# Head channels in the even rows of a slot: one transfer for the slots of four heads

## The chip, the cores and the metric

The kernel runs on one core of a Trainium2 chip. The metric is the device time of one execution in microseconds (us); the time before is the median of three runs. A profile is one execution recorded by the hardware profiler; its span runs from the first to the last recorded instruction.

## The reference

The layer has four sequences of 1024 positions with 256 channels. Cut to what matters here:

```python
def attention(x, w_attn, w_proj):             # 16 heads of 16 channels
    q, k, v = split(x @ w_attn.T)
    att = einsum("bhqd,bhkd->bhqk", q, k) / sqrt(16)
    att = att + where(rel <= 0, slope[h] * rel, -inf)   # rel = key position - query position
    return (softmax(att) @ v) @ w_proj.T

x = x + attention(layernorm(x))
x = x + encoder_layer(layernorm(x))  # attention over the 4 sequences at each position,
                                     # router, one of 8 experts per row, two norms
```

The change lies in the first attention, in how a score `q k` gets its position term `slope * rel`.

## The kernel before

**Slots.** A group is four of the 16 heads. For each group there is a tile `slots[g]` of 128 partitions; each head has 32 of them, its slot. The first 256 columns are queries, the other 1024 are keys. The first 16 rows of a slot (D = 16) hold the head's channels. The rows after them hold what the scores add: row 16 carries the key's position against a constant in the queries, row 17 a constant against the query's position, and rows 18 to 25 one row for each block of 128 positions, by which scores of the second half of a block's keys with the first half of its queries, all above the diagonal, are pushed down. One matmul over the 32 rows of a slot gives a head's scores with the position term included. `key_rows` and `query_rows` write these rows with VectorE and GpSimd operations on all 128 partitions; they use small tables made at the start: `at_row` (1 in row 16), `is_one` (1 in row 17), `at_block`, `steep`, `k_by` (from the slopes) and `q_by` (the slopes in row 17, loaded by four small transfers).

**Units and stages.** The work is cut into chunks of 256 queries (c = 0 to 3) for each of the four sequences; a unit is one chunk of one sequence, and in the last chunk 128 queries, so there are 20 units. A unit needs the keys of its own and all earlier chunks, so stage c has 256(c+1) key columns. For each unit and group, `score` makes the scores on TensorE (tile `sk`), ScalarE takes the exponential (`p`), GpSimd cuts the diagonal block, and `weigh` multiplies by the values (`pv`).

**Filling a slot.** `project_qk` makes queries and keys of two groups at once (tile `qkp`, copied by VectorE into `kq`) and stores them to `k_of` in device memory. `fill_slots(u, g)` then copies the channels of the four heads into the slots, straight from `kq` in stage 0 and from `k_of` afterwards. The 64 channel rows of a group are consecutive in the source, but in the slots there are gaps of 16 rows after every 16, so it takes four transfers, one for each head. They are issued on SP, for the first unit every second one on ScalarE. A fill of group g for unit u+1 stands in the program right after the last scores of group g in unit u.

**Order.** The order of instructions is written by the program: slots E and D between the scores take the projections and the next part of the layer, with due times from a small cost table. Each engine works in its own order. SP's queue holds, in program order, the stores of `k` and `y`, the fills, the loads of `x`, and for each unit after its attention a chain: load the softmax sums (`load_sums`), VectorE inverts them (`invert`), store them (`r`), load them spread over channels (`load_inverse`, tile `su`), VectorE multiplies (`divide`, tile `yc`), then `project` multiplies by `wp` on TensorE. In stage 0 the `y` stores are issued by ScalarE.

PSUM has four pairs of banks that go round: scores, products and projections take them in turn, so a score waits until the reader of an earlier tile in its pair is done.

Of the kernel before, what the change touches and what calls it, by code (L numbers as in the profile page):

```python
# [33 lines left out]
ALU = mybir.AluOpType  # L34
# [3 lines left out]
P = 128  # L38
B, T, C = 4, 1024, 256
H, D, E = 16, 16, 8  # L40
S = 32
G = H // 4
# [4 lines left out]
W = 256  # L47
# [34 lines left out]
IDENT, MASK_Q, MASK_K, K_ROWS, SLOPES, Q_ROW, IOTA, EARLIER = (  # L82
    0, P, 2 * P, 3 * P, 3 * P + T, 3 * P + T + G, 3 * P + T + G + 1, 3 * P + T + G + 1 + E,
)
# [522 lines left out]
def fast_layer(ctx: ExitStack, tc: tile.TileContext, odd, x, wq, wk, wv, wp, w_in, w_out, w_r,  # L607
# [26 lines left out]
    nc = Core(tc.nc, told)  # L634
# [14 lines left out]
    def const(name, shape, dtype=F32, into=keep):  # L649
        return into.tile(shape, dtype, tag=name, name=name)  # L650
# [45 lines left out]
    con = lambda at, n=1: low_con[:, at - SLOPES:at - SLOPES + n]  # L696
# [7 lines left out]
    load_x(2)  # L704
    q_by = const("q_by", [P, G])
    nc.vector.memset(q_by, 0.0)
    for j in range(4):
        r = j * S + D
        nc.scalar.dma_start(q_by[r + 1:r + 2], consts[r:r + 1, SLOPES:SLOPES + G])
    mask = fact.tile([P, P], F32, tag="sc", name="mask")  # L710
    nc.scalar.dma_start(mask, consts[:, MASK_Q:MASK_Q + P])
    wp_sb = load("wp", wp, [P, CC, C], into=ends)
# [17 lines left out]

    minus_half = const("minus_half", [P, 1])
    nc.vector.memset(minus_half, -0.5)
    at_row = con(Q_ROW)
    number_i = const("number_i", [P, 1], I32)
    nc.gpsimd.iota(number_i, pattern=[[0, 1]], base=0, channel_multiplier=1)
    pos = fact.tile([P, T], F32, tag="pr", name="pos")
# [11 lines left out]
    number = const("number", [P, 1])  # L748
    nc.vector.tensor_copy(number, number_i)
    own_e = const("own_e", [P, 1])  # L750
    nc.vector.tensor_copy(own_e, own_e_i)
    is_one = const("is_one", [P, 1])
    nc.vector.tensor_scalar(is_one, number, float(D + 1), None, ALU.is_equal)


    at_block = const("at_block", [P, NT])
    steep = const("steep", [P, NT])
    for i in range(NT):
        nc.vector.tensor_scalar(at_block[:, i:i + 1], number, float(D + 2 + i), None, ALU.is_equal)
    nc.vector.tensor_scalar(steep, at_block, STEEP, None, ALU.mult)  # L760
    other = const("other", [P, 1])
    k_by = const("k_by", [P, G])
    nc.vector.tensor_scalar(other, at_row, 4.0, None, ALU.mult)
    nc.vector.tensor_scalar(k_by, con(SLOPES, G), other, None, ALU.mult)
    nc.vector.tensor_scalar(other, at_row, -1.0, 1.0, ALU.mult, ALU.add)


    slots = [const(f"slots{g}", [P, W + T], into=pad) for g in range(G)]
# [11 lines left out]
    def query_rows(c, g):  # L780

        qt = slots[g][:, :W]
        nc.vector.tensor_scalar(qt, q_pos, float(c * W), other, ALU.add, ALU.mult)
        nc.vector.tensor_scalar(qt, qt, at_row, q_by[:, g:g + 1], ALU.add, ALU.mult)
        if g == 0:
            for n in range(PC):
                early = qt[:, n * P:n * P + P // 2]
                i = PC * c + n
                nc.vector.tensor_scalar(early, early, steep[:, i:i + 1], None, ALU.add)
# [47 lines left out]
    k_of = [dram.tile([C, W + T], F32, tag=f"k_{b}", name=f"k_{b}") for b in range(B)]  # L837
# [10 lines left out]
    sums, at = [], 0  # L848
# [4 lines left out]
    held = {}  # L853
# [8 lines left out]
    def issue_stores(*keys, age=None):  # L862
        due = [it for it in stores if it[0] in keys or age is not None and it[1] >= age]
        for it in due:
            stores.remove(it)
            it[2]()
# [77 lines left out]
    def fill_slots(u, g):  # L944

        n, i, _ = units[u]
        c, b = batches[n]
        if b == 0 and c and i == 0:
            query_rows(c, g)
        for j in range(4):  # L950
            at, row_ = slice(j * S, j * S + D), (4 * g + j) * D
            n_cols = W + (c + 1) * W
            issue_stores(("k", n, g // 2))
            src = k_of[b][row_:row_ + D, :n_cols]
            if c == 0:
                row_ = (4 * (g % 2) + j) * D
                src = held["kq", n, g // 2][row_:row_ + D].rearrange("p k w -> p (k w)")
            queue = nc.scalar if u == 0 and j % 2 else nc.sync
            queue.dma_start(slots[g][at, :n_cols], src)

    def blocks_of(u, r):

# [159 lines left out]
    slot_sum = const("slot_sum", [P, P])  # L1122
    nc.gpsimd.memset(slot_sum, 0.0)
    for j in range(4):
        at = slice(j * S, (j + 1) * S)
        nc.gpsimd.tensor_copy(slot_sum[at, at], at_row[at].to_broadcast([S, S]))

    def load_slotted():
        held["wp"] = []
# [918 lines left out]
    queue, running = [], []  # L2048
# [93 lines left out]
    def slots_of(n, half):  # L2142
        return lambda: [fill_slots(n, 2 * half + k) for k in range(2)]

    for u, (n, i, size) in enumerate(units):
        c, b = batches[n]
# [77 lines left out]
    for g in range(G):  # L2224
        at_E(-8, lambda g=g: key_rows(g, 0, W, nc.vector if g else nc.gpsimd))
        at_E(1 + g, lambda g=g: key_rows(g, W, T, nc.vector if g else nc.gpsimd))
    at_E(-5, lambda: [fill_slots(0, g) for g in range(2)])
    at_E(-3, lambda: [fill_slots(0, g) for g in range(2, G)])
    at_E(4, prepare)
    at_E(6, part.prepare)  # L2230
# [152 lines left out]
    def begin(it):  # L2383
        if it.kind == "DQ" and ("qkv",) in held or it.kind[1:] == "C" and part.placed < NT - 1:
            return 1e9
        return max(it.ready, free[engine_of[it.kind[0]]])
# [27 lines left out]
    while threads:  # L2414
# [4 lines left out]
        at, _, it = min((begin(it) + FIRST_BY * n, n, it) for n, it in enumerate(threads))  # L2419
# [14 lines left out]
    n = 0  # L2434
# [11 lines left out]
@with_exitstack  # L2446
def tile_layer(ctx: ExitStack, tc: tile.TileContext, *args):
    nc = tc.nc
    flag = ctx.enter_context(tc.tile_pool(name="flag", bufs=1))
    odd = flag.tile([P, 1], I32, tag="odd", name="odd")  # L2450
    fast_layer(tc, odd, *args)
    again = nc.values_load(
        odd[0:1, 0:1], min_val=0, max_val=1,
        skip_runtime_bounds_check_because="a comparison's result",
    )
    with tc.If(again > 0):
        general_layer(tc, *args)
# [75 lines left out]
```

## Time and profile before

| | |
|---|---|
| median of three runs | 805.2 us (803.28 to 805.44) |
| the profiled execution | 802.74 us, span 801.0 us |
| TensorE busy | 710.5 us (89%) |
| VectorE, ScalarE, GpSimd busy | 521.5, 433.0, 254.1 us |
| mean granted TensorE clock | 0.966 |
| transfers into slots on SP | 56 of 32 KB from `kq`; 64 of 48 KB, 64 of 64 KB, 128 of 80 KB from `k_of` |
| transfers into slots on ScalarE | 8 of 32 KB from `kq` |

In the profile's lines a group is given as line, engine, operation, output<-inputs and count; busy time and idle time before it follow. "L588" is a helper through which all instructions of TensorE, VectorE and ScalarE are issued, so these are told apart by their tiles. Names ending in q (SPq, ACTq) are an engine's sequencer: it waits or issues a transfer. A line of the chain of waits gives a start, a duration and what it was; a transfer's duration there runs from its issue to its landing.

### The profile page before, as it was taken

To read this page: it belongs to the slowest core of one execution; us is meant where nothing else is said; L and a number is where in the kernel's file an instruction comes from. 1 tells how busy PE (TensorE), PEld (TensorE's weight loads), DVE (VectorE), ACT (ScalarE), POOL (GpSimd) and SP (SyncE) were. 2 spreads that over 40 slices of the span, in tenths; PEclk is the share of its full clock that TensorE was granted. 3 is DMA by queue.
4 is the path that set the end of the run, shared out by engine and by line. 5 is a ranking of instruction groups with operands and counts; after the bars stand their busy time and mean duration, and the time that the engine had idled before them with its cause. 6 is when DMAs were issued, how large, how long until landed. Compare 5 with 4: busy or idle time off the path is not lost.

```text
span 801.0 us, 22678 instructions
## 1 busy us (share of the span) xinstructions
PE 710.5 (89%) x9029; PEld 538.2 (67%) x9029; DVE 521.5 (65%) x1282; ACT 433.0 (54%) x663; POOL 254.1 (32%) x360
## 2 busy tenths in 40 slices
PE   4889869999998999999889999899998687979993
PEld 3666656666666666666568877578777466868882
DVE  7245324747887574889672338588689788865553
ACT  1455525745556565556547657458467163646650
POOL 5443202312222120114221211123112230788874
PEclk9799979999999999999999999999999999999997
DMA  7344444343344332325354545246431660444420
GB/s 221 98 155 139 144 136 136 121 117 110 84 141 126 109 123 76 100 80 155 89 161 139 134 142 170 76 132 173 122 116 52 186 255 27 135 130 123 127 86 26
DMA packets 75220, 99.57 MB, mean 124 GB/s; under 512 B 19496, under 2 KB 58723, under 8 KB 74596
## 3 DMA queue, kind: packets, MB, share of 16 engines
q1 hardware_dynamic: 62272, 67.84, 28.8%
q10 hardware_dynamic: 7972, 16.05, 6.4%
q0 software_dynamic: 4864, 14.16, 5.9%
q8 instruction: 74, 1.21, 0.7%
q14 instruction: 38, 0.31, 0.1%
HBM read 61.55 MB, written 35.12 MB: 121 GB/s over the span
## 4 chain that ended last, share of the span: by engine, by line
PE 53%; DVE 20%; DMA 8%; issue 7%; POOL 6%; ACT 3%; SPq 1%; ACTq 0%; POOLq 0%; DVEq 0%
PE sk L588 14%; PE pv L588 11%; PE qkvp L588 9%; PE qkp L588 6%; PE vp L588 5%; DVE pv L588 4%; POOL given L1852 3%; ACT p L588 2%; PE oe L588 2%; DVE sc L588 2%; PE op L588 2%; DVE pr L588 1%; PE ao L588 1%; DVE u L588 1%; DMA out_dram<-o,out_rows 1%
## 5 line engine op out<-in xcount | busy, mean ns | idle before, releaser
L588 ACT ACTIVATE p<-sk 128x1024 f32<-128x1024 f32 (+1 forms) x320 | 287.4, 940 | 157.8 <-PE sk L588 138.5
L1006 POOL TENSOR_SCALAR_AFFINE_SELECT p<-p 128x512 f32<-128x512 f32 (+1 forms) x160 | 105.6, 664 | 426.9 <-ACT p L588 424.9
L588 PE MATMUL sk<-slots 32*128 32x128 f32 (+1 forms) x3456 | 180.8, 328 | 23.5 <-issue 9.5
L588 PEld LDWEIGHTS sk<-slots 32*128 32x128 f32 x3456 | 137.0, 188 | 65.8 <-issue 31.8
L588 PE MATMUL pv<-p,v 128*32 128x128 f32 (+1 forms) x3456 | 143.4, 313 | 10.3 <-ACT p L588 4.0
L588 PEld LDWEIGHTS pv<-p,v 128*32 128x32 f32 x3456 | 95.6, 110 | 47.9 <-ACT p L588 7.8
L588 PE MATMUL qkvp<-w_in,ut 128*128 128x264 f32 (+1 forms) x240 | 85.1, 493 | 0.2 <-ACT ut L588 0.2
L588 PEld LDWEIGHTS qkvp<-w_in,ut 128*128 128x128 f32 x240 | 43.1, 193 | 29.6 <-issue 24.8
L588 PE MATMUL qkp<-xt,wqk 128*128 128x256 f32 x224 | 56.2, 396 | 0.2 <-ACT p L588 0.2
L588 PEld LDWEIGHTS qkp<-xt,wqk 128*128 128x128 f32 x224 | 41.4, 193 | 10.9 <-issue 3.3
L588 ACT ACTIVATE mt<-mtp,columns 128x128 f32<-128x128 f32 x76 | 30.7, 455 | 30.6 <-PE mtp L588 30.6
L588 DVE COPY kq<-qkp 128x512 f32<-128x512 f32 x28 | 19.1, 683 | 43.1 <-PE qkp L588 42.7
L588 PE MATMUL hid<-mt,w 128*128 128x128 f32 x304 | 44.6, 283 | 2.6 <-ACT ge L588 1.7
L1852 POOL DMA_INDIRECT given<-rows,rows x38 | 42.1, 1108 | 9.7 <-issue 8.5
L588 PEld LDWEIGHTS hid<-mt,w 128*128 128x128 f32 x304 | 40.0, 191 | 3.8 <-ACT ge L588 2.2
L588 DVE COPY vr<-qkvp 128x264 f32<-128x264 f32 x28 | 12.1, 432 | 46.3 <-PE qkvp L588 46.3
L1967 POOL DMA_INDIRECT out_dram<-o,out_rows x38 | 39.2, 1033 | 8.7 <-issue 5.9
L588 ACT COPY qkv<-qkvp 128x512 f32<-128x512 f32 x28 | 16.4, 585 | 46.8 <-PE qkvp L588 46.7
L588 PE MATMUL oe<-w,ge 128*128 (+1 forms) x152 | 40.0, 386 | 0.0
L588 DVE TENSOR_TENSOR pv<-vr,sc 128x1024 f32<-128x1024 f32 x32 | 39.6, 1238 | 0.3
L588 DVE TENSOR_REDUCE sc<-pr 128x64 f32<-128x1024 f32 x32 | 39.0, 1220 | 1.1
L588 DVE TENSOR_TENSOR pr<-qkv 128x1024 f32<-128x1024 f32 x32 | 39.2, 1224 | 0.5 <-ACT qkv L588 0.2
(317 smaller groups left out, 1038.4 us busy)
## 6 DMA issues: line engine op xcount, KB each, us to landing
slots<-k SPq DMA_DIRECT2D x128, 80.0 KB
k<-kq SPq DMA_DIRECT2D x32, 256.0 KB
v<-v ACTq DMA_DIRECT2D x4, 1152.0 KB
x<-in_x_dram SPq DMA_DIRECT2D x16, 256.0 KB
y<-yt SPq DMA_DIRECT2D x16, 256.0 KB
rows<-x SPq DMA_DIRECT2D x32, 128.0 KB
slots<-k SPq DMA_DIRECT2D x64, 64.0 KB
rows<-u SPq DMA_DIRECT2D x8, 512.0 KB
```

Source lines behind the costliest of these rows:

```text
L588: ins = made(*args, **kwargs)
L1006: nc.gpsimd.affine_select(blocks, blocks, pattern=[[0, 2], [0, size], [1, P]], compare_op=ALU.is_ge, fill=0.0, base=0, channel_multiplier=-1,)
L1852: nc.gpsimd.indirect_dma_start(out=self.hx, out_offset=None, in_=t.rows_of, in_offset=bass.IndirectOffsetOnAxis(ap=t.rows_[:, self.j:self. ...
L1967: ins = nc.gpsimd.indirect_dma_start(out=out.rearrange("t n c -> (t n) c"), out_offset=bass.IndirectOffsetOnAxis(ap=t.table.out_rows[:, t. ...
```

## The change

The channels of a head move to the even rows of its slot, row 2d for channel d, and what the scores add moves to odd rows: the key position to row 1, the constant and the slopes to row 3, the eight blocks to rows 5 to 19. The channels of four heads are then 64 rows at a step of two in the slots and 64 consecutive rows in the source, and `fill_slots` makes one transfer. In the first unit the transfers go by group, not by head, to SP and ScalarE in turn. The tables follow: `at_row` is now made by a comparison on VectorE (the old one, a column of the constants, stays as `sum_row` for the sums), the slopes are loaded into rows 1 (`slopes`, used for `k_by`) and 3 (`q_by`) by two transfers of four rows each in place of four transfers of one row.

```diff
-    for j in range(4):
-        r = j * S + D
-        nc.scalar.dma_start(q_by[r + 1:r + 2], consts[r:r + 1, SLOPES:SLOPES + G])
+    slopes = const("slopes", [P, G])
+    nc.vector.memset(slopes, 0.0)
+    for t, r in ((slopes, 1), (q_by, 3)):
+        nc.scalar.dma_start(t[r:P:S], consts[D:P:S, SLOPES:SLOPES + G])
...
-    at_row = con(Q_ROW)
+    sum_row = con(Q_ROW)
...
-    is_one = const("is_one", [P, 1])
-    nc.vector.tensor_scalar(is_one, number, float(D + 1), None, ALU.is_equal)
+    at_row, is_one = const("at_row", [P, 1]), const("is_one", [P, 1])
+    nc.vector.tensor_scalar(at_row, number, 1.0, None, ALU.is_equal)
+    nc.vector.tensor_scalar(is_one, number, 3.0, None, ALU.is_equal)
...
-        nc.vector.tensor_scalar(at_block[:, i:i + 1], number, float(D + 2 + i), None, ALU.is_equal)
+        nc.vector.tensor_scalar(at_block[:, i:i + 1], number, float(5 + 2 * i), None, ALU.is_equal)
...
-    nc.vector.tensor_scalar(k_by, con(SLOPES, G), other, None, ALU.mult)
+    nc.vector.tensor_scalar(k_by, slopes, other, None, ALU.mult)
...
-        for j in range(4):
-            at, row_ = slice(j * S, j * S + D), (4 * g + j) * D
-            n_cols = W + (c + 1) * W
-            issue_stores(("k", n, g // 2))
-            src = k_of[b][row_:row_ + D, :n_cols]
-            if c == 0:
-                row_ = (4 * (g % 2) + j) * D
-                src = held["kq", n, g // 2][row_:row_ + D].rearrange("p k w -> p (k w)")
-            queue = nc.scalar if u == 0 and j % 2 else nc.sync
-            queue.dma_start(slots[g][at, :n_cols], src)
+        n_cols = W + (c + 1) * W
+        issue_stores(("k", n, g // 2))
+        src = k_of[b][4 * g * D:4 * (g + 1) * D, :n_cols]
+        if c == 0:
+            row_ = 4 * (g % 2) * D
+            src = held["kq", n, g // 2][row_:row_ + 4 * D].rearrange("p k w -> p (k w)")
+        queue = nc.scalar if u == 0 and g % 2 else nc.sync
+        queue.dma_start(slots[g][0:P:2, :n_cols], src)
```

More of the change, by code (lines that the diff above doesn't have):

```diff
@@ L1125, in fast_layer @@
         at = slice(j * S, (j + 1) * S)
-        nc.gpsimd.tensor_copy(slot_sum[at, at], at_row[at].to_broadcast([S, S]))
+        nc.gpsimd.tensor_copy(slot_sum[at, at], sum_row[at].to_broadcast([S, S]))
     def load_slotted():
```

## The prediction

> **What bounds the kernel now.** I read the slices of the page first, then the groups, the table of waits, the chain of waits, and last the timeline of single engines around every hole in TensorE's work.
>
> ```profile
> PE   4889869999998999999889999899998687979993
> PEclk9799979999999999999999999999999999999997
> ACT xt L588 <- DMA slots<-kq: 11.7, 1, 11.7
> DVE yc L588 <- DMA su<-r: 18.4, 5, 11.6
> SPq L959 <- PE sk L588: 120.8, 53, 12.4
> L959 SPq DMA_DIRECT2D slots<-k x256: 302/370/1787, 83.0 to 600.3; - x128
> L959 SPq DMA_DIRECT2D slots<-kq x56: 507/539/2519, 17.2 to 74.1; - x56
> ```
>
> TensorE (the first line; a slice is 20 us) is full from about 110 to 600 us and has its holes before 110 us and after 600. The clock line shows lower digits in the same early slices. The three lines of the waits name what is late: transfers into the slots at the start, and once a load of `su` that kept VectorE waiting 11.6 us. The last two lines are the issues that the change touches: 312 on SP, each 0.37 or 0.54 us long, in one queue with every store and load of the attention.
>
> The chain of waits, and the timelines of SP, VectorE and TensorE, at the holes:
>
> ```profile
> 2.31 5.12 DMA q_by<-in_consts_dram
> 24.26 1.65 PE sk L588 x10
> 68.60 3.61 DMA k<-kq
> 72.29 0.39 ACTq L588
> 73.65 1.45 PE sk L588 x10
> 83.43 2.15 DMA slots<-k
> 86.52 1.96 PE sk L588 x15
> ...
> 69.59 5.04 SPq L959 DMA_DIRECT2D slots<-kq  x8
> 83.00 4.40 SPq L959 DMA_DIRECT2D slots<-k  x8
> 96.04 4.30 SPq L959 DMA_DIRECT2D slots<-k  x8
> 100.44 0.37 SPq L1085 DMA_DIRECT2D r<-inverse  x1
> 103.29 1.33 SPq L1096 DMA_DIRECT2D su<-r  x2
> 107.00 0.69 DVE L588 TENSOR_TENSOR yc<-yc,su 128x512 f32<-128x512 f32 x1 [11.62 <-DMA su<-r]
> 107.61 0.68 DVE L588 COPY kq<-qkp 128x512 f32<-128x512 f32 x1
> 108.39 2.20 PE L588 MATMUL sk<-slots 32*128 32x256 f32 x16 [6.76 <-issue]
> ```
>
> Three holes hang on SP's queue. (1) At 72 us ScalarE sits at the issue of a `y` store until the `k` store of 68.60 has landed (72.21), though the two share no data: in the program as built the transfers of SP and ScalarE take eight completion semaphores in turn, and an issue waits until the holder before it has landed. Its exponentials start at 72.79, and TensorE stands 1.71 us for a bank. (2) At 84.45 TensorE stands 2.06 us until the first fills of the second stage land; SP came to them late, through 16 fills and their neighbours. (3) At 101.63 TensorE stands 6.76 us: `r` is issued only behind eight fills (100.44), `su` after it has landed, the division on VectorE waits for `su`, and the copy of `kq` queued behind it frees the bank that the scores need.
>
> **The change, part by part.** *SP's queue.* 256 fills from DRAM at a pitch of 0.43 us and 56 from `kq` at 0.63 become 64 and 14: 192 x 0.43 + 42 x 0.63 = 109 us less of issuing. By itself that is worth nothing, since SP waits 121 us for scores anyway; it counts where SP is behind, which is in the three places. An issue of 64 rows does not occur before; the nearest are those of 16 rows (0.37, 0.54) and the stores of `k`, 128 rows (0.33 to 0.53); I take 0.45. Its landing lies between the 2.15 us of a 16-row fill and the 3.61 us of a `k` store that was delayed; I take 2.5 us, against 1.3 + 2.15 = 3.5 us until the last of four staggered fills.
>
> *Hole 1.* With 8 fills fewer between them, the holder before the `y` store landed long ago. 1.71 us of standing go. The clock goes with them: the granted clock was 0.50 from 73.9 to 77.3, in which 32 `pv` took 2.60 us (1.51 elsewhere) and 12 `sk` 1.45 (0.70): 1.8 us more. Gain 3.5.
>
> *Hole 2.* From 61 to 83 us SP issues 16 fills (10 us); as four at 0.5 they leave SP some 6 us ahead, less what `kq`'s second half makes it wait (copied at 66.5), so about 4: the fills are issued near 76.5 and land near 79, while TensorE, 3.5 us ahead, asks at 81. Gain 2.06 of standing and, at 0.50 of the clock after it, 1.0 on `sk` (1.96 for 0.94) and 1.25 on `vp` (3.24 for 1.99): 4.3.
>
> *Hole 3.* I walk SP on: fills done 77; three `b_bf` 79.3, `sums` and `yc` 81.2, three `in_bf` 83.1, `k` store 83.6, landed 86; two fills 86.7; `r` 87, landed 89; `su` lands 92.3; division 93, copy of `kq` 93.7. TensorE, with its own work between from the timeline (93.30 to 101.63, moved by the 7.8 us of holes 1 and 2), asks at 93.8. So next to nothing of the 6.76 stays; I leave 0.3. In the before, 104.6 to 114.9 ran at 0.50: `sk` 2.20 for 0.94, eight `vp` 3.78 for 1.99, four transposes 0.97 for 0.60, 3.4 us. Gain 9.9. If `su` is later than I walk, each us of it costs one.
>
> By the Trainium skill (TensorE: Matmul & The Clock Gate, section Why this matters for your kernels) only gaps over about 3 us bring the slow clock. The trace does not agree: holes of 1.71 and 2.06 us were each followed by 3.4 us at 0.50. By that rule the sum would be about 4 us smaller.
>
> *The start.* In unit 0 the last fill of group 0 is held until 21.16 by the semaphore of a `b_rows` transfer and lands at 24.2; the scores end at 25.9. After, that group is one transfer, and ScalarE issues two fills for eight (6.2 us there). Against it stands a new wait: `k_by` now reads `slopes`, which comes where the first `q_by` row came, behind the 512 KB of `wk` on ScalarE's queue, and that row landed at 7.43; `k_by` ran at 3.82. Behind it on VectorE are queued `row_no`, `places`, the statistics of `x_0` and then `xn`, on which the first transposes wait. They move from 7.45 to about 10.4, 2.9 us, and all up to the transposes at 19.14 with them; these end at 23.4, the fill (issued 20.2) has landed by 22.7, the scores run to 25.05. Gain 0.9; bounds: 2.9 gain if `slopes` does not lie behind `wk`, 2.1 loss if it lands 3 us later than `q_by` did.
>
> *With one answer.* `at_row` by a comparison (0.15 us) and a memset of `slopes` (0.06) lie in VectorE's 1.15 us of waiting for `low_con`; without that cover they cost 0.2. Two issues fewer on ScalarE at 2.31 gain nothing, the table load has 2 us of slack. Comparisons with 5 + 2i cost what those with 18 + i did. `slot_sum` reads the old constant column. Matmuls keep 32 rows and their order, so TensorE's own work stays.
>
> *Later.* The holes at 211, 384 and 416 us wait for VectorE's own work. At 500.1 (2.72 us) the fills lie behind a 1152 KB load of `v`; all four landed just after it, and one transfer will too. The tail after 620 us starts earlier by the whole gain.
>
> Sum: 3.5 + 4.3 + 9.9 + 0.9 = 18.6. I take off 1.6 for new small waits, since the 6.8 us of hole 3 were also time in which the other engines caught up (the groups show VectorE fed by TensorE with single waits up to 9.6 us): 17. The profiled execution took 802.74 us (span 801.0 and 1.7 around it), so 785.7. It lies 2.5 under the median of 805.2 and 0.5 under the fastest run; the median should come to 788.
>
> **The rivals.** *Part of it (793 to 802).* The copies of `kq` are held by VectorE's own chain rather than by `su`, or hole 2 moves on to the transfer of one `k` store; then hole 3 gives 4 or less and the sum is 3 to 12. For: VectorE waits in that stretch for several transfers in turn (`sums` 4.8, `b_bf` 2.1). Against: in hole 3 it was idle for 11.6 us.
>
> *Nothing (803 to 807).* SP only runs ahead to the next score it must wait for. For: 120.8 us of such waits. The Trainium skill (DMA: Bandwidth & Descriptors, section Issuing engines are not separate DMA queues) states that the time to issue is usually small relative to the transfer. Here eight issues take 4.3 us against 2.15 us of one landing, so it is not small in this queue. Against: no wait for a score stands between the fills and `r` in hole 3.
>
> *Slower (806 to 810).* The wait of `k_by`. It costs 2.9 us before the first transpose; it decides if the holes at 72 to 108 us are not SP's: then the start stands alone, and it turns from a gain of 0.9 to a loss once `slopes` lands after 8.3 instead of 7.43; 3 us later makes it 2.1, and the half clock after the longer hole up to 3 more. For: nothing covers it. Against: the first scores waited until 24.26 for fills.
>
> *The change does not do what it says*: 64 partitions at a step of two could be served as slowly as four transfers one after the other, 4 x 2.15 = 8.6 us to land. Fills have a unit's time (14 us in the first stage, over 25 later) after the score that frees the slot, so only holes 2 and 3 would stay: 797 to 802, inside the first rival.
>
> **How the numbers follow.** Forecast (783 to 793) 0.63; part 0.20; nothing 0.06; slower 0.11. A measurement of this kernel can tell about 0.3%, 2.4 us, from no change, so faster begins under 802.8: 0.83, within 0.06, slower 0.11. The range reaches from 781, if the start gains its 2.9 and `su` and all else fit, to 802, the end of the partial case.
>
> **What would show it.** In the profile after: 64 + 14 fills on SP at 0.3 to 0.6 us; `k_by` at about 7.5 and the first `xn` at about 10.4; the first scores done by 25; no hole over 1 us in TensorE between 60 and 100 us, and a granted clock of 1.00 there; the score that stood at 108.39 near 93; SP's waits for scores above 120.8 us, since it arrives earlier. The prediction is wrong if hole 3 stays above 3 us, if a new hole of that size opens before 200 us, or if fills land later than 4 us after their issue outside the big `v` loads.

## The result: 785.8 us for 805.3

The changed kernel takes 785.76 us (median of four runs, 784.45 to 786.16), the kernel before 805.32 on the same chip (four runs, 803.28 to 806.1): 19.5 us less, a ratio of 0.976 (95% interval 0.974 to 0.978). The forecast was 788 in a range of 781 to 802. The profiled execution took 784.45 us (span 782.7), 18.3 less than that of before.

The page of after, its slices (one of 40 is now 19.6 us):

```profile
PE   3889899999999999998989999999997879879992
PEclk9999899999999999998999999999999898999997
```

TensorE's 6 in the sixth slice is a 9 now and the 8 in the fifth has stayed; the clock's 7 in the second and in the sixth slice are gone, and an 8 in the fifth is new (80 to 87 us). By windows of 60 to 110 us TensorE was busy 39.5 us at a mean granted clock of 0.88 before, and 47.9 us at 0.93 after. From the tables of waits of after (all in us: in total, how often, the longest):

```profile
ACT p L588 <- DMA b_bf<-pieces: 6.3, 2, 4.6
DVE yc L588 <- DMA su<-r: 6.0, 4, 3.3
SPq L961 <- PE sk L588: 149.7, 39, 13.7
```

VectorE's wait for `su` is down from 18.4 to 6.0 us, and SP waits longer for scores (149.7 for 120.8), as it does when it comes earlier. The first line is new: exponentials that wait 4.6 us for a bias transfer. The fills, by the line that issues them (shortest, median and longest issue in ns):

```profile
L961 SPq DMA_DIRECT2D slots<-k x64: 450/487/753, 75.3 to 576.0; - x64
L961 SPq DMA_DIRECT2D slots<-kq x14: 462/519/708, 19.9 to 64.7; - x14
```

The timelines of SP, ScalarE, VectorE and TensorE at the places of holes 2 and 3:

```profile
76.55 2.57 SPq L1505 DMA_DIRECT2D b_bf<-pieces  x3
85.58 1.13 SPq L961 DMA_DIRECT2D slots<-k  x2
86.80 0.54 SPq L1087 DMA_DIRECT2D r<-inverse  x1
89.38 1.30 SPq L1098 DMA_DIRECT2D su<-r  x2
...
79.78 0.34 ACTq L588 DMA_DIRECT2D v<-v  x1
80.22 1.51 ACT L588 ACTIVATE p<-sk 128x768 f32<-128x768 f32 x2 [4.61 <-DMA b_bf<-pieces]
...
93.05 0.69 DVE L588 TENSOR_TENSOR yc<-yc,su 128x512 f32<-128x512 f32 x1 [1.53 <-DMA su<-r]
94.36 0.69 DVE L588 COPY kq<-qkp 128x512 f32<-128x512 f32 x1 [0.62 <-PE qkp L588]
...
81.08 2.08 PE L588 MATMUL sk<-slots 32*128 32x256 f32 x12 [2.07 <-ACT p L588]
97.22 1.15 PE L588 MATMUL sk<-slots 32*128 32x256 f32 x16
```

Hole 3 is closed: the last line is the score that stood at 108.39 behind 6.76 us of idle time; it comes 2.2 us after the copy of `kq` has ended (94.36 + 0.69) and waits for nothing. The hole that waited for fills is gone, but four matmuls further on there is one of the same 2.07 us with another cause (called hole 2 all the same below). A load of `v` on ScalarE (`load_values`, for the second stage), issued at 79.78, takes over the completion semaphore of a `b_bf` transfer that lands at 79.76, and the exponentials queued behind that load start at 80.22. TensorE waits for the bank that they read.

Counting TensorE's matmuls (9029 in each profile) shows where the time came from. The table gives how much earlier the n-th starts after than before; the predicted terms stand beside their stretches. The last column is the same count on a second profile of each kernel (`before2` and `after2` below):

| up to matmul | earlier by, us | of this stretch | predicted | of this stretch, second pair |
|---|---|---|---|---|
| 400 (start; 59.8 us after) | 2.0 | 2.0 | 0.9 | -0.8 |
| 600 (hole 1) | 6.1 | 4.0 | 3.5 | 4.4 |
| 700 (hole 2) | 4.4 | -1.7 | 4.3 | -0.3 |
| 900 (hole 3) | 14.3 | 10.0 | 9.9 | 8.0 |
| 5000 (447.7 us after) | 16.8 | 2.4 | no gain, less 1.6 | 3.8 |
| 6000 (the hole at 500 us before) | 21.4 | 4.6 | 0 | 5.5 |
| 9000 (tail) | 18.3 | -3.1 | 0 | 0.8 |

Two executions stand behind each pair, so a row carries the accidents of both. Hole 1, hole 3 and the hole at 500 us give a gain in both pairs, hole 2 in neither; the start and the tail change sign.

### The profile page after: what moved, and what is told of

Read it like the earlier page. It is cut to its first block, busy times and chain, and to the rows that moved or that the text cites. A ratio compares the mean times of both kernels' runs of the same rounds, so it can differ in the third digit from the quotient of the medians.

```text
span 782.7 us, 22121 instructions
## 1 busy us (share of the span) xinstructions
PE 705.6 (90%) x9029; PEld 535.4 (68%) x9029; DVE 523.5 (67%) x1284; ACT 433.3 (55%) x663; POOL 256.9 (33%) x360
## 5 line engine op out<-in xcount | busy, mean ns | idle before, releaser
L1008 POOL TENSOR_SCALAR_AFFINE_SELECT p<-p 128x512 f32<-128x512 f32 (+1 forms) x160 | 107.8, 678 | 401.1 <-ACT p L588 399.0
L588 PE MATMUL sk<-slots 32*128 32x128 f32 (+1 forms) x3456 | 177.6, 327 | 8.9 <-DVE kq L588 4.2
L588 PEld LDWEIGHTS sk<-slots 32*128 32x128 f32 x3456 | 134.6, 187 | 51.0 <-issue 21.2
L588 PE MATMUL qkvp<-w_in,ut 128*128 128x264 f32 (+1 forms) x240 | 83.5, 486 | 0.2 <-ACT ut L588 0.2
```

The source lines that it names most:

```text
L588: ins = made(*args, **kwargs)
L1008: nc.gpsimd.affine_select(blocks, blocks, pattern=[[0, 2], [0, size], [1, P]], compare_op=ALU.is_ge, fill=0.0, base=0, channel_multiplier=-1,)
```

## The experiments

The runs were made in three groups, each on one chip, and the kernel before was slower or more scattered there than above (medians 813.7, 807.7 and 804.9 us). So a ratio is to the before of its own group, and kernels of one group are compared with each other.

**Four transfers in the new layout.** This keeps rows, tables and the two transfers saved at the start, and undoes only the number of fills. `e2_unit4`, `e3_unit16` and `e9_from5` are the same edit with `u == 4`, `u == 16` and `u >= 5` in place of `True`.

```diff
+        if True:
+            for j in range(4):
+                queue = nc.scalar if u == 0 and j % 2 else nc.sync
+                queue.dma_start(slots[g][j * S:(j + 1) * S:2, :n_cols], src[j * D:(j + 1) * D])
+            return
         queue = nc.scalar if u == 0 and g % 2 else nc.sync
         queue.dma_start(slots[g][0:P:2, :n_cols], src)
```

> The kernel after, with its rows and tables, but with four transfers of 16 rows for a group again (in the first unit every second one on ScalarE). If the gain is the number of issues, SP's queue is as full as before: 803 to 807 us, a ratio of 1.000 to the kernel before, and the 6.8 us hole near 102 us and the 2.7 us hole near 500 us are back. If it comes from where the rows lie, from the tables or from the two transfers saved at the start, it stays at 784 to 790.

Measured: 820.3 us, a ratio of 1.009 (1.006 to 1.012). The gain is the number of issues, and the new layout with as many issues as before is a loss, which neither theory had. The line of the fills in its profile:

```profile
L963 SPq DMA_DIRECT2D slots<-k x256: 485/539/1726, 79.5 to 611.6; - x128
```

An issue of 16 rows at a step of two takes 0.54 us where one of 16 adjacent rows took 0.37 (median, from `k_of`): 256 x 0.17 = 43 us more in SP's queue. That this is the whole of the loss is not shown. The three early holes are back, with 2.4, 1.8 and 7.35 us, and new holes of 2.6 and 4.0 us opened at 136 and 243 us. One issue of 64 rows at a step of two takes 0.49, less than one of 16.

> The kernel after, with four transfers for a group in unit 4 alone (the first of the second stage): 12 issues more of 240, some 5 us of SP's time between 75 and 90 us. If the holes of 84 and 102 us come from SP's backlog at this place, su lands about 5 us later (near 98 instead of 92.97), the division and the copy of kq with it; TensorE asks for the bank at about 97, so a hole of about 3 us opens there, and the clock falls after it: 4 to 8 us more than after, 790 to 794 (ratio 0.981 to 0.986). If issues cost the same wherever they stand, 12 of 240 cost 5% of 19.5 us, 1 us: 786.8 (0.977).

Measured: 803.9 us, 0.987 (0.981 to 0.993), 11 us more than `e3_unit16` in the same group (792.9), which stands for after there; the first theory had 4 to 8. VectorE and TensorE, at the place of hole 3:

```profile
103.44 0.69 DVE L588 TENSOR_TENSOR yc<-yc,su 128x512 f32<-128x512 f32 x1 [14.07 <-DMA su<-r]
...
96.75 1.54 PE L588 MATMUL sk<-slots 32*128 32x256 f32 x12 [3.59 <-ACT p L588]
104.83 2.20 PE L588 MATMUL sk<-slots 32*128 32x256 f32 x16 [3.88 <-issue]
```

`su` landed at 103.3, 10 us later than after, not 5: beside the issues themselves SP stood from 89.1 to 93.1 until a `k` store had landed. The 3.59 us are a `y` store of ScalarE that waited for the landing of one of these fills (95.12). From matmul 600 to 900 this kernel lost 10 us against `e3_unit16`. Twelve issues of 240 cost about half of the whole gain at this place (11 of the 20.8 us between before and `e3_unit16`), where the count alone gives 5%; the price is that of the place. Hole 2 was not there: the load of `v` went out at 76.11, ahead of the bias transfers.

> The kernel after, with four transfers for a group in unit 16 alone, the one whose fills stood beside a 1152 KB load of v at 493 us before. If four small transfers beside the load make both slow (8.8 us for the load before, 5.5 after), the load beside the second group's fills takes 8 to 9 us again, a hole of 2 to 3 us opens near 482 us, and the time is 3 to 5 us more than after: 789 to 791 (ratio 0.979 to 0.982). If it was only the chance position of the load among other transfers, as the prediction's 'one transfer will too' has it, nothing changes by over 1 us: 785 to 787.

Measured: 792.9 us, 0.973 (0.969 to 0.977), not to be told from after. The load of `v` took 5.4 us beside four fills, and no hole opened at 480 us. Four transfers at this unit alone do not make the hole.

> The kernel after, with four transfers for a group from unit 5 on (after 97 us) and one in units 0 to 4. If only the queue before 110 us carries the gain, nearly all of it stays: 0 to 5 us more than after (ratio 0.976 to 0.983). If the later issues cost too, as the run with four transfers everywhere suggests (it lost some 12 us against after up to 108 us and 14 to 15 more behind that, its issues taking 0.54 us each where those of before took 0.37), it gives 12 to 16 us back (0.991 to 0.997).

Measured: 798.7 us, 0.991 (0.989 to 0.994): of the 2.4% about 1.5 points are lost, as the second theory said. Its profile follows that of after, taken again (below), within 2 us up to matmul 1000 and is 14 us behind at the end. But this does not price the later fills of before: these took 0.37 us each, and between 110 and 480 us before has no hole over 1 us that after does not have too.

**The start.**

```diff
     low_con = load("low_con", consts[:, SLOPES:], [P, N_CONST - SLOPES], nc.scalar)
     con = lambda at, n=1: low_con[:, at - SLOPES:at - SLOPES + n]
+    q_by = const("q_by", [P, G])
+    nc.vector.memset(q_by, 0.0)
+    slopes = const("slopes", [P, G])
+    nc.vector.memset(slopes, 0.0)
+    for t, r in ((slopes, 1), (q_by, 3)):
+        nc.scalar.dma_start(t[r:P:S], consts[D:P:S, SLOPES:SLOPES + G])
     load_x(0)
...
     load_x(2)
-    q_by = const("q_by", [P, G])
...
```

> The kernel after, with the two small loads of slopes and q_by issued right behind low_con on ScalarE's queue, ahead of ident and wk. k_by then runs near 4 us instead of 7.46 and the first xn near 7.5 instead of 10.19. If the path of the start goes through xn, as the prediction's start term has it, the first scores come 2 to 2.7 us earlier: 783 to 784 (ratio 0.973). If the path goes through the loads of the weights or of x, nothing is gained: 785 to 786.5.

Measured: 791.8 us (790.0 to 794.0), 0.972 (0.968 to 0.976), against 792.9 for `e3_unit16` of its group; the times alone do not tell it from no gain. The traces do. VectorE of after, and then of this kernel:

```profile
7.46 0.23 DVE L588 TENSOR_SCALAR k_by<-slopes,other 128x4 f32<-128x4 f32 x1 [4.83 <-DMA slopes<-in_consts_dram]
10.19 1.02 DVE L588 TENSOR_SCALAR xn<-x,mv_x,rstd_x 128x256 f32<-128x256 f32 x2 [0.84 <-POOL rstd_x L819]
```

```profile
5.26 0.23 DVE L588 TENSOR_SCALAR k_by<-slopes,other 128x4 f32<-128x4 f32 x1 [2.63 <-DMA slopes<-in_consts_dram]
8.00 1.02 DVE L588 TENSOR_SCALAR xn<-x,mv_x,rstd_x 128x256 f32<-128x256 f32 x2 [0.85 <-POOL rstd_x L819]
```

`xn` comes 2.2 us earlier, and matmul 100 with it (31.0 us; 33.3 in `e3_unit16`; below, 30.8 in `e7_both` with the same edit and 33.2 in `e6_bias` without). The new wait is real; the early load takes back 2.2 us of it, not all, as `slopes` still lands at 5.2.

**Hole 2.** First after once more, for its group:

> The kernel after once more, on the chip of the three that follow, so that these can be set against it. 0.9758 to the kernel before again, within 0.5%; hole 2 (2 us near 79 us) and the half clock after it are there again, hole 3 is not.

Measured: 787.7 us (787.05 to 788.12), 0.977 (0.973 to 0.981). Hole 2 is there (1.9 us, and half clock), hole 3 is not.

> The kernel after, with the stores of v and y in the first stage on SP (put off like those of the later stages) in place of ScalarE. If hole 2 is ScalarE standing at the issue of the v store at 79.78 until a b_bf transfer has landed, with the exponentials behind it, the hole of 2.07 us near 79 us goes and with it some 2 us of half clock: 3 to 4 us less than after (ratio 0.971 to 0.973). If the exponentials wait for something else there, the hole stays, and SP has eleven issues more (4 to 5 us): 0 to 3 us more than after (0.976 to 0.980).

```diff
-        if c:
-            store(("v", b), lambda: nc.sync.dma_start(to, own))
-        else:
-            nc.scalar.dma_start(to, own)
+        store(("v", b), lambda: nc.sync.dma_start(to, own))
```

and the same for the stores of `y`. Measured: 790.3 us (787.1 to 792.3), 0.980 (0.975 to 0.984), 2.7 more than `after2`. The transfer at 79.78, which the expectation calls a store, is a load of `v`, and this edit leaves it on ScalarE. ScalarE and TensorE of this kernel:

```profile
78.62 0.37 ACTq L588 DMA_DIRECT2D v<-v  x1
79.09 1.51 ACT L588 ACTIVATE p<-sk 128x768 f32<-128x768 f32 x2 [4.93 <-PE pv L588]
...
79.95 1.13 PE L588 MATMUL sk<-slots 32*128 32x256 f32 x12 [0.81 <-ACT p L588]
97.74 2.79 PE L588 MATMUL sk<-slots 32*128 32x256 f32 x16 [4.75 <-ACT turned_w L588]
```

With the stores gone from ScalarE the order of the semaphores is another: the load takes over that of a fill, which lands at 78.54, 1.2 us earlier than the `b_bf` transfer did, and hole 2 shrinks to 0.81 us. So the load waits for whichever transfer held its semaphore; whether the stores matter is not tested. Hole 3 opened again with 4.75 us. TensorE, held less by hole 2, asked for the bank at 93.0 (after: 97.2). SP, with the stores of `v` and `y` ahead of the next fills, issued `r` at 87.80 and `su` at 91.77 (after: 86.80 and 89.38), and the copy of `kq` ended at 96.77. Last came ScalarE's copy `turned_w`, which ended at 97.69, behind another load of `v` whose semaphore a `yc` transfer had held until 96.7.

> The kernel after, with the splitting of the biases (twelve small transfers on SP, and VectorE's work for them) moved from 70 to 84 us and later to 105 to 130 us. If these transfers are what ScalarE's stores wait for (landings at 73.55, 79.76 and 84.69), hole 2 goes as in the run before, and SP is some 6 us freer at that place, so r and su come earlier too: 3 to 5 us less than after (ratio 0.970 to 0.972). If any transfer of SP takes their place in the rotation, hole 2 stays, or a new one opens near 110 us: within 1 us of after (0.975 to 0.977).

```diff
-    for k, at in enumerate((-6, 12, 13, 14, 23)):
+    for k, at in enumerate((-6, 24, 25, 26, 27)):
         at_E(at, lambda k=k: prepare_biases(k))
```

Measured: 783.5 us (779.1 to 786.7), 0.972 (0.968 to 0.976), 4.2 less than `after2`. ScalarE's load of `v`, SP and TensorE:

```profile
74.77 0.34 ACTq L588 DMA_DIRECT2D v<-v  x1
...
83.03 0.54 SPq L1087 DMA_DIRECT2D r<-inverse  x1
...
90.41 0.92 PE L588 MATMUL sk<-slots 32*128 32x256 f32 x12 [0.80 <-ACT p L588]
92.98 1.15 PE L588 MATMUL sk<-slots 32*128 32x256 f32 x16
```

No hole over 0.8 us is left between 60 and 110 us, and the granted clock of that window is 1.00. From matmul 500 to 700 it gained 4.6 us on `after2`: the size that the prediction gave to hole 2 (4.3), from another source. The score that stood at 108.39 comes at 92.98.

> The two loads of slopes and q_by early (as in the run e4) and the splitting of the biases late (as in the run e6) together, as the version that should beat after. The start gave 2.2 us up to the first scores and the biases are thought to give 3 to 5: if these add up, 5 to 7 us less than after (ratio 0.967 to 0.970). If a faster start only meets the next wait, or hole 2 stays, 0 to 3 us less (0.972 to 0.976).

Measured: 782.0 us (781.2 to 784.5), 0.970 (0.966 to 0.974), 5.7 less than `after2` and the lowest median of all, though `e6_bias`, whose runs reach from 779.1 to 786.7, is not to be told from it; all its runs lie below all of `after2`. Up to matmul 1000 it was 8.4 us ahead of `after2` (start 4.7, hole 2 the rest), of which the end shows 5.3. Of the 4.7 at the start the early loads give some 2.4: `e6_bias`, without them, was 2.2 ahead of `after2` at matmul 100 as well.

**Before, with the biases late.** The edit of `e6_bias`, made in the kernel before; and before itself for its trace.

> The kernel before, all its 320 fills kept, with the splitting of the biases moved from 70 to 84 us and later to 105 to 130 us, as in the run e6. Nine issues, some 6 us, leave SP's queue ahead of r. If hole 3 is SP's backlog, r comes some 5 us earlier (near 95 instead of 100.44), hole 3 shrinks from 6.8 us to 1 to 2 and hole 2 goes: 6 to 10 us less than before (ratio 0.987 to 0.993), with no fill saved. If it is the number or the shape of the fills by which the change gains, the time stays at that of before (0.998 to 1.003).

Measured: 797.8 us, 0.9905 (0.987 to 0.994), inside the first theory's bounds: 7 us without one fill saved.

```profile
97.22 0.37 SPq L1085 DMA_DIRECT2D r<-inverse  x1
...
75.14 0.92 PE L588 MATMUL sk<-slots 32*128 32x256 f32 x12 [2.53 <-ACT p L588]
104.54 2.20 PE L588 MATMUL sk<-slots 32*128 32x256 f32 x16 [4.67 <-issue]
```

`r` came 3.2 us earlier than in before (100.44), not 5: SP waited for a `k` store ahead of the eight fills. Hole 3 kept 4.67 us, more than expected, and hole 2 went; hole 1 stayed, with all its fills in place.

> The kernel before once more, for its trace. If the holes at 72, 84, 102 and 500 us belong to the program, all four are there again within 1 us of their lengths (1.7, 2.1, 6.8, 2.7). If the one at 500 us was an accident of that one execution (a load of v that took 8.8 us), it is missing, and the load takes 5 to 6 us.

Measured: one run, 809.2 us. The four holes are there again, 2.11, 1.19, 6.73 and 3.47 us; the load of `v` near 500 us took 7.8 us. All four belong to the program.

## Why the prediction was right, and where not

*SP's queue, hole 3: right in its cause, with some luck in its size.* The walk gave `r` at 87, `su` landing at 92.3, the division at 93; measured 86.80, 92.97 and 93.05. The term was 9.9 us and the table shows 10.0, in the second pair 8.0. `e2_unit4` brings the hole back with twelve issues and `e10_before_bias` takes part of it away with no fill saved, so the cause is the backlog in front of `r`, as stated. One premise was off: TensorE asked at 97.2, not at 93.8, because hole 2 had stayed, and that covered a remainder. By the walk's own times the copy of `kq`, started at 93.7 and 0.68 us long, ends 0.6 us after TensorE asks, not 0.3. Had TensorE asked at 93.0, as in `e5_stores` and `e6_bias`, a division at 93.05 and the copy behind it would have left about 1.4 us (an estimate from these rows). `e6_bias` has no such hole, but there `r` went out at 83.03, 3.8 us earlier than in after.

*Hole 1: right in mechanism, 4.0 us for 3.5.* In the traces of after no hole stands there, and it stays in `e10_before_bias`, which keeps the fills, and comes back in `e1_four`. One reading was off: the 0.70 us set against 1.45 for 12 `sk` is the row of four; twelve take 0.92 at full clock (`e6_bias`, 90.41), so the term should have been 3.3.

*Hole 2: wrong.* The failed step is "the fills are issued near 76.5 and land near 79, while TensorE, 3.5 us ahead, asks at 81. Gain 2.06 of standing". The fills were issued at 75.3 and 75.9 and landed by 79.6, near what it said, and no matmul waited for them. What failed is the silent step from "the fills are there" to "TensorE goes on". With the fills out of the way, SP issued the next `b_bf` transfers at 76.55, and ScalarE's load of `v` drew the semaphore of one of them. The prediction had named this very mechanism for hole 1 and did not walk ScalarE's other transfers through the same rotation. In place of +4.3 came -1.7 (-0.3 in the second pair): a hole of the same length, then 6.8 us at a clock of 0.50 instead of 3.4. Three of the prediction's own signs fail with it: a hole over 1 us stands between 60 and 100 us, the clock there is not 1.00, and the score of 108.39 came at 97.22 and not near 93. Where the load came clear of the bias transfers (`e2_unit4`, `e6_bias`), this hole is gone.

*The clock after a hole.* The holes of 2.07 us (after) and 1.89 us (`after2`) were again followed by half clock, and those of 0.80 and 0.81 us (`e6_bias`, `e5_stores`) by none in that place. The length alone does not decide it: a hole of 1.19 us (`before2`, at 83 us) was followed by 3.4 us of half clock, and holes of 1.25 us (`e9_from5`, hole 2) and 2.38 us (`e1_four`, at 68 us) by none. So the part of a term that stands for the clock, half of hole 1 and of hole 2 in the sum, can come or fail to come. The Trainium skill (TensorE: Matmul & The Clock Gate, section Why this matters for your kernels) advises against gaps over about 3 us; the shorter holes named here, like those in the trace of before, do not agree with that as a limit.

*The start: right in its parts, its size not settled.* `k_by` ran at 7.46 and `xn` at 10.19 as forecast (7.5 and 10.4). The first scores ended at 24.45 for 25.05. But matmul 100 came at 33.1 us in after and 35.4 in `after2`, at 35.5 in before and 33.9 in `before2`: two executions of one kernel differ by 2 us here, so neither 0.9 nor 2.0 can be held against the other. In `after2` the load of `slopes` landed at 8.42 for 7.36, and all behind it moved.

*New small waits: not seen.* For the 1.6 us taken off nothing shows. Between matmuls 900 and 5000 after gained 2.4 us on before, but against each other the two profiles of after and the two of before give -0.2 to 6.4, so no size is shown.

*Later: wrong.* "All four landed just after it, and one transfer will too" held in the letter, since fill and load of `v` still land together, but both land 3 us earlier. The load took 8.8, 7.8 and 7.6 us in the three profiles with the old rows (before, `before2`, `e10_before_bias`; holes 2.7, 3.5 and 2.1 us) and 5.0 to 5.7 us in all seven with one transfer in this unit, with no hole. Why is open: four fills at a step of two in this unit alone left it at 5.4 us, four from unit 5 on gave 6.4, four everywhere 7.5 with a hole of 1.4. The number of transfers beside the load does not settle it, and whether adjacent rows do was not tried, since the layout can't be changed for one unit.

*The tail.* In after it gave 3.1 us back, while `after2` ended as far ahead of `before2` as it was at matmul 6000 (21 us), and `e4_slopes` and `e3_unit16` lost 7 to 9 us there against `after2`. It differs that much from execution to execution, and nothing of it is put down to the change.

*The rivals.* That 64 rows at a step of two are served like four transfers in turn (8.6 us) is refuted: they landed in 2.4 us (median, first stage) to 3.4 (last stage). Some later ones took over 4 us, nearly all beside a load of `v`; two did not stand beside one (5.0 us at 379, 4.5 at 469), and no hole followed them. That SP only runs ahead is refuted by the ratio; of the 109 us of issues saved 29 did go into longer waits for scores. The slower case needed the start to stand alone, and it did not.

So the total agreed (17 forecast, 18.3 in the profiles, 19.5 in the medians) partly because errors offset: hole 2 came out 6.0 us below the forecast and the tail 3.1; the hole at 500 us came out 4.6 above it, the stretch before that 4.0, the start and hole 1 together 1.7. That the two sides cancel is luck.

## What to carry to other kernels

Price a saved DMA issue by what stands behind it in its queue at that place, not by its length: here twelve of 240 issues ahead of one short chain cost about half the gain. When a queue empties, walk every in-order engine that shares its completion semaphores again, for an engine that only issues a transfer can stop until another queue's transfer has landed (ScalarE here for 4.6 us). A change of layout and a change of the number of transfers should be priced apart: the layout with four transfers a group made this kernel 0.9% slower, and only together with the single transfer was it a gain. And before an experiment moves an instruction, make sure which one the trace shows: `v<-v` stands for stores and loads alike.

## What was not expected of the hardware

An issue of 16 partitions at a step of two took 0.54 us on SP, and of 16 adjacent ones 0.37 (each the median of 256, from device memory; from `kq` both took 0.54); one of 64 at a step of two took 0.49 and landed 0.4 to 0.8 us later than those of 16 adjacent ones (medians 2.41 for 2.04 us in the first stage, 2.77 for 1.95 in the second).
